# Windowed attention in the last layer: each pair of 7x7 windows placed at partitions 0 and 64, with one image row of windows as the unit of work

## The chip, the cores and the metric

The kernel runs on one core of one Trainium2 chip. A core has five engines that run on their own instruction streams: TensorE (PE in the profile, with its weight loads shown apart as PEld), VectorE (DVE), ScalarE (ACT), GpSimd (POOL) and SyncE (SP), which here only issues DMA transfers. They meet through semaphores. The metric is the device time of one execution in microseconds (us); lower is better.

## The reference

The program is four layers on a tensor x of 4 images, 56 x 56 positions, 256 channels, each of the form x = x + f(groupnorm(x)). The change concerns the last layer only, which is attention in shifted 7 x 7 windows with 8 heads of 32 channels:

```python
xs = jnp.roll(x, (-3, -3), axis=(1, 2))
xw = xs.reshape(B, 8, 7, 8, 7, C).transpose(0, 1, 3, 2, 4, 5).reshape(B * 64, 49, C)
qkv = (xw @ qkv_weight.T + qkv_bias).reshape(B * 64, 49, 3, 8, 32).transpose(2, 0, 3, 1, 4)
q, k, v = qkv[0] * 32 ** -0.5, qkv[1], qkv[2]
attn = jnp.einsum('whnd,whmd->whnm', q, k) + bias          # one 49 x 49 block for a window and a head
attn = softmax(attn + mask_of_the_window)
out = jnp.einsum('whnm,whmd->wnhd', attn, v).reshape(B * 64, 49, C) @ proj_weight.T + proj_bias
return roll_back(out)                                       # and x + this
```

All of it is in 32-bit floats. A window has 49 positions, an image has 8 x 8 windows, and the 4 images together have 32 rows of 8 windows.

## The kernel before

The four layers run one after another; the last one, `layer3`, fills the span from about 3430 us to its end at 3978 us. Inside it the program order of TensorE, VectorE, ScalarE and GpSimd is the order in which the source issues their instructions (`run(3, ...)` fixes these four engines); only the DMA queue is left to the planner. Activations lie with the channels on partitions, 2 halves of 128 channels by 392 positions for a row of 8 windows.

A row r goes through these steps:

- `prepare(r)` normalises the loaded x into `xn`: six VectorE instructions (line 939) and one small copy on ScalarE (line 2023).
- `project_rows(r)` makes keys and queries. Each of its four steps (keys, queries for the first 128 channels, then for the second) is two TensorE matmuls of 392 columns into a one-bank PSUM tile `ps_m` (line 945), and one ScalarE instruction that takes the result out (line 2035 for keys, 2039 for queries). There are two `ps_m` tiles, used in turn, so the third product in a sequence can't start before the first has been taken out.
- `values(r)` makes the values in two steps, a=0 with two position tiles and a=1 mostly with one (line 971); VectorE adds the bias (line 975), the result goes to DRAM, and `gather` reads it back by windows.
- attention, in `attend_quads`. Its unit is one row and one group of four heads (`quad(r, hq)`, 64 units). Two windows of 49 positions are handled as one piece of 98 by 98. The logits (line 1012) have the 98 keys on the partitions of PSUM: four heads stand in four 32-row groups of TensorE, so a matmul uses 32 rows and 98 columns. Half of every 98 x 98 piece belongs to two different windows and is masked off. Heads 0 and 1 go to PSUM tile s0, heads 2 and 3 to s1. ScalarE exponentiates s1 (line 1016) and GpSimd multiplies it by an exponentiated mask (line 1019); VectorE adds the mask to s0 (line 1017) and ScalarE exponentiates the sum (line 1018). The products with the values and with a matrix of ones (line 1027) use 98 rows and 32 columns, with the four heads in four column groups, and fill the PSUM tile `o`, of which there is one. `finish` takes the reciprocal of the sums (line 2075), lets GpSimd add it up for a later check (`seen`, line 985), and multiplies (line 2077).
- `project_out(r)` makes two more products like those of the projections, taken out by ScalarE (line 2097) and added to x on GpSimd (line 2099).

The loop of `attend_quads` is a pipeline of one unit. For a unit it issues the logits and the mask and exponentials, then `done()`, which is `finish` of the unit whose products came last, then `fill`, which is a share of the projections of row r+1, the values of row r+2, the output of row r-2 and the preparing of row r+3, and then the products of the unit before. The fill of a unit is one step of `project_out`, two of `project_rows` and one of `values`; the second unit of a row adds `prepare`. So on VectorE the mask addition of a unit stands ahead of the reciprocal.

The additive masks of this layer are made earlier in the run by `table_steps`, kept in DRAM (`m3d`) and loaded once into `m3`.

Of the kernel before, what the change touches and what calls it, by code (L numbers as in the profile page):

```python
# [24 lines left out]
FP = mybir.dt.float32  # L25
# [6 lines left out]
NIMG = 4  # L32
S = 56
T = S * S
C = 256
# [11 lines left out]
G2 = S // 2  # L47
WN = 49
WC = 8 * WN
GN_EPS = 1e-5  # L50
LN_EPS = 1e-5
TINY = 1e-12
# [84 lines left out]
def _constants():  # L137
# [47 lines left out]
    for lastrow in range(2):  # L185
        for lastpair in range(2):
            for w in range(2):
# [3 lines left out]
                if lastpair and w == 1:  # L191
# [2 lines left out]
                m3[sl, 2 * lastrow + lastpair, sl] = np.where(  # L194
                    part[:, None] != part[None], -100.0, 0.0)
    c["c_m3"] = m3
    return c


# [631 lines left out]
def direct_blocks(ctx: ExitStack, tc: tile.TileContext, d: dict, watch):  # L831
# [161 lines left out]

    def attend_quads(pool, units):

        def logits(w):
            nk, nq, nu = w["nk"], w["nq"], len(w["pieces"])
            w["first"]()
            s = [psum_tile(f"s{a}", 1, 2) for a in range(2)]
            for u, (k, q, *_) in enumerate(w["pieces"]):  # L1010
                for j in range(4):
                    nc.tensor.matmul(s[j // 2][:nk, j % 2, u * nq:(u + 1) * nq], lhsT=k(j), rhs=q(j),  # L1012
                                     start=True, stop=True)
            w["e"] = [pool.tile([P, 2, w["width"]], FP, tag=f"e{a}", name=f"e{a}", bufs=2) for a in range(2)]
            ev = [e[:nk, :, :nu * nq] for e in w["e"]]
            nc.scalar.activation(ev[1], s[1][:nk, :, :nu * nq], AF.Exp, accum_out=w.get("sum"))  # L1016
            nc.vector.tensor_tensor(ev[0], s[0][:nk, :, :nu * nq], w["mask"].to_broadcast([nk, 2, nu * nq]), ALU.add)
            nc.scalar.activation(ev[0], ev[0], AF.Exp)
            nc.gpsimd.tensor_tensor(ev[1], ev[1], w["emask"].to_broadcast([nk, 2, nu * nq]), ALU.mult)  # L1019

        def products(w):
            nk, nq = w["nk"], w["nq"]
            for k in range(2):
                for u, (_, _, v, start, stop) in enumerate(w["pieces"]):
                    po = w["o"](k, u)
                    for j in range(4):
                        nc.tensor.matmul(  # L1027
                            po[j * HD:(j + 1) * HD], lhsT=ones[:nk, :HD] if k else v(j),
                            rhs=w["e"][j // 2][:nk, j % 2, u * nq:(u + 1) * nq], start=start, stop=stop)

        held, done = None, no_step
        for w in units:
            logits(w)
            done()
            w["fill"]()
            if held:
                products(held)
                done = held["done"]
            held = w
        done()  # L1040
        products(held)
        held["done"]()


    def attend_pairs(pool, units):
# [870 lines left out]

    m3d = dram.tile([98, 2, NH, 4, 98], FP, name="m3d")

    def table_steps(big, pool):

# [8 lines left out]
        tab = big.tile([P, 2, NH], FP, name="tab")  # L1931
        nc.sync.dma_start(out=tab[:, 0], in_=d["table"][:P])
        nc.sync.dma_start(out=tab[:NR - P, 1], in_=d["table"][P:])
        t3 = big.tile([98, 4, 98], FP, name="t3")
        nc.sync.dma_start(out=t3, in_=d["c_m3"])
        base = big.tile([98, NH, WN], FP, name="base")

        def look_up(q0):
            idxf = pool.tile([P, NQ, WN], FP, tag="idxf", name="idxf")
            nc.vector.tensor_copy(idxf, idx[:, q0:q0 + NQ, :])  # L1940
            hot = pool.tile([P, 2, NQ * WN], FP, tag="hot", name="hot")
            for a, n in ((0, P), (1, NR - P)):
                nc.vector.tensor_scalar(hot[:n, a, :], idxf[:n].rearrange("p q k -> p (q k)"),
                                        rowf[:n, a:a + 1], None, ALU.is_equal)
            pb = ps_m()
            for a, n in ((0, P), (1, NR - P)):
                nc.tensor.matmul(pb[:NH, :NQ * WN], lhsT=tab[:n, a, :], rhs=hot[:n, a, :], start=(a == 0), stop=(a == 1))
            tb = pool.tile([NH, NQ, 98], FP, tag="tb", name="tb")
            for w in range(2):
                nc.vector.tensor_copy(tb[:, :, w * WN:(w + 1) * WN], pb[:NH, :NQ * WN].rearrange("p (q k) -> p q k", k=WN))  # L1950
            pt = ps_m()
            for q in range(NQ):
                nc.tensor.transpose(pt[:98, q * NH:(q + 1) * NH], tb[:, q, :], ident[:NH, :NH])
            nc.vector.tensor_copy(base[:, :, q0:q0 + NQ], pt[:98, :NQ * NH].rearrange("p (q h) -> p h q", h=NH))

        def mask(ty):
            m = pool.tile([98, NH, 98], FP, tag="m3", name="m3")
            for w in range(2):
                sl = slice(w * WN, (w + 1) * WN)
                nc.vector.tensor_tensor(m[:, :, sl], base, t3[:, ty:ty + 1, sl].to_broadcast([98, NH, WN]), ALU.add)  # L1960
            mv = m.rearrange("p (q j) k -> p q j k", j=4)[:, :, 2:4]
            nc.scalar.activation(mv, mv, AF.Exp)
            for pair in [3] if ty % 2 else range(3):
                nc.sync.dma_start(out=m3d[:, ty // 2, :, pair, :], in_=m)

        return [lambda q=q: look_up(q) for q in range(0, WN, NQ)] + [lambda ty=ty: mask(ty) for ty in range(4)]

# [11 lines left out]
    def layer3(early, big, pool, brief):  # L1979
# [16 lines left out]

        load(0)
        w_qkv = weight(early, "wqkv3", 3 * C)
        m3 = big.tile([98, 2, NH, 4 * 98], FP, name="m3l")
        nc.sync.dma_start(out=m3, in_=m3d.rearrange("p a h w k -> p a h (w k)"))  # L2000
        w_p = weight(pool, "wp3", C)

        def parts(win, x):
# [22 lines left out]
        def project_rows(r):  # L2026
            at = left(r % 8, WC)
            xn = xns.pop(r)[:, :, at:at + WC]
            qT = pool.tile([P, CC, WC], FP, tag="q", name="q3")
            kT = pool.tile([P, CC, WC], FP, tag="k", name="k3")  # L2030
            qk[r] = qT, kT

            def keys(m):
                pm = project(w_qkv, C + m * P, lambda h: xn[:, h, :], WC)
                nc.scalar.activation(kT[:, m, :], pm, AF.Identity, bias=bk3[:, m:m + 1])

            def queries(m):
                pm = project(w_qkv, m * P, lambda h: xn[:, h, :], WC)
                nc.scalar.activation(qT[:, m, :], pm, AF.Identity, bias=qbias[:, 2, m:m + 1], scale=SCALE)

            return [lambda f=f, m=m: f(m) for m in range(2) for f in (keys, queries)]

        def gather(r):

            b, c = divmod(r, 8)
            vs[r] = pool.tile([98, 4, C], FP, tag="v", name="v3")
            nc.sync.dma_start(out=vs[r], in_=vd[b][c * WC:(c + 1) * WC, :].rearrange("(k p) c -> p k c", p=98))

        def values(r):

# [9 lines left out]
                    gather(r)  # L2060
            return [lambda a=a: step(a) for a in range(2)]

        def quad(r, hq):
            b, wr = divmod(r, 8)
            qT, kT = qk[r]
            box = {}

            def output(k, u):
                if k + u == 0:
                    box["o"] = psum_tile("o", 1, 2)  # L2070
                return box["o"][:, k, u * 98:(u + 1) * 98]

            def finish():
                rs = pool.tile([P, WC], FP, tag="rs", name="rs3")
                nc.vector.reciprocal(rs, box["o"][:, 1, :WC])  # L2075
                seen(rs)
                nc.vector.scalar_tensor_tensor(attns[r][:, hq, :], box["o"][:, 0, :WC], 1.0, rs, ALU.mult, ALU.mult,
                                               accum_out=watch[2][:, 2 * r + hq:2 * r + hq + 1])

            def piece(u):  # L2080
                sl = slice(u * 98, (u + 1) * 98)
                return (lambda j: kT[hr(j), hq, sl], lambda j: qT[hr(j), hq, sl],
                        lambda j: vs[r][:, u, (4 * hq + j) * HD:(4 * hq + j + 1) * HD], True, True)

            mk = m3[:, wr // 7, 4 * hq:4 * hq + 4, :]
            i = 2 * (NIMG * 8 + r) + hq
            return dict(pieces=[piece(u) for u in range(4)], nk=98, nq=98, width=WC, mask=mk[:, 0:2, :],
                        emask=mk[:, 2:4, :], sum=watch[2][:98, i:i + 1], o=output, first=no_step, done=finish)

        def project_out(r):  # L2090
            x = pool.tile([P, CC, WC], FP, tag="xr", name="xr3")
# [12 lines left out]
        def stream():  # L2104
            n = NIMG * 8
            for r in range(n):
# [1 line left out]
                rows = lazily(project_rows, r + 1, 4) if r + 1 < n else []  # L2108
                ahead_values = lazily(values, r + 2, 2) if r + 2 < n else []
                out = project_out(r - 2) if r > 1 else []  # L2110
                for hq in range(CC):
                    steps = out[hq:hq + 1] + rows[2 * hq:2 * hq + 2] + ahead_values[hq:hq + 1]
                    if hq and r + 3 < n:
                        steps.append(lambda r=r: prepare(r + 3))
                    steps.append(step_stats)
                    w = quad(r, hq)
                    w["fill"] = lambda steps=steps: [f() for f in steps]
                    yield w

        prepare(0)  # L2120
        prepare(1)
# [3 lines left out]
        for step in project_rows(0):  # L2125
            step()
        prepare(2)
        attend_quads(pool, stream())
        for r in range(NIMG * 8 - 2, NIMG * 8):
            for step in project_out(r):  # L2130
                step()

# [122 lines left out]
```

## Time and profile before

| what | value |
|---|---|
| device time, median of 3 runs | 3989.01 us (3976.07 to 3992.41) |
| span of the profiled execution, first to last instruction | 3977.8 us |
| TensorE busy over the span | 3814.5 us (96%) |
| VectorE / ScalarE / GpSimd busy | 60% / 35% / 44% |
| the last layer | about 3430 to 3978 us |
| its steady part | 3461 to 3924 us |
| one row of windows there | 15.6 us |

The span counts from the first to the last instruction; the device time has some 11 us more around it. The chain of work that ended last names, for each stretch of time, the instruction on which the end depended. A line of the timeline gives start, duration, engine, source line, operation, tiles and count; in brackets stands how long the engine was idle before it and what released it. One 32-bit matmul of the source appears as two matmul records and two weight loads[...].

### The profile page before, as it was taken

The page shows a single profiled execution, that of the slowest core. Times are in us where ns is not written, and L with a number is a line of the kernel's source. Part 1 is how long each engine was busy: PE and PEld are TensorE (multiplying, and loading weights), DVE is VectorE, ACT ScalarE, POOL GpSimd, SP SyncE. Part 2 cuts the span into 40 slices and gives each one's busy share as a digit, 9 for nine tenths or more (in the row PEclk, how much of TensorE's full clock was granted, in tenths as well). Part 3 has the DMA queues.
Part 4 walks back from the last instruction along what each step waited for, and adds up shares of the span by engine and source line. Part 5 has one row for each costly group of instructions (what it writes and reads, how often), then busy time and mean ns, then how long its engine had stood idle before and what let it go on. Part 6 is the DMA issues. An engine that isn't in the chain of part 4 may idle for free. (4 is left out here: it accounts for less than half of the span.)

```text
span 3977.8 us, 92350 instructions
## 1 busy us (share of the span) xinstructions
PE 3814.5 (96%) x38871; PEld 2707.4 (68%) x38871; DVE 2372.2 (60%) x4431; ACT 1381.2 (35%) x2927; POOL 1745.8 (44%) x1883
## 2 busy tenths in 40 slices
PE   7999999889999999999999999999999999899998
PEld 4566666557777677776777767776676666566765
DVE  6777777734345544445444553446788887666665
ACT  3455545422222222222222222222555555344443
POOL 3566767721123312233112331123677777555554
PEclk9899999989999999999999999999999999999999
DMA  8343333320000100001000000001344443434442
GB/s 270 104 134 119 113 120 104 99 104 1 24 19 24 40 6 15 20 25 35 6 24 15 25 24 10 10 10 56 111 125 126 125 121 111 157 120 135 127 128 93
DMA packets 268659, 301.84 MB, mean 76 GB/s; under 512 B 25926, under 2 KB 260584, under 8 KB 267752
## 3 DMA queue, kind: packets, MB, share of 16 engines
q1 hardware_dynamic: 267946, 295.76, 23.9%
q8 instruction: 308, 5.05, 0.5%
q14 instruction: 117, 0.96, 0.1%
q10 hardware_dynamic: 288, 0.08, 0.0%
HBM read 203.39 MB, written 92.37 MB: 74 GB/s over the span
## 5 line engine op out<-in xcount | busy, mean ns | idle before, releaser
L1441 DVE TENSOR_TENSOR acc<-acc,ps_v 128x257 f32<-128x257 f32 x1104 | 463.4, 423 | 718.7 <-PE ps_v L1519 690.7
L1519 PE MATMUL ps_v<-xw,e 128*128 128x257 f32 x2208 | 612.6, 382 | 1.2 <-DVE acc L1441 1.2
L1514 PE MATMUL ps_o<-xw,at 128*128 128x257 f32 x2208 | 609.0, 379 | 0.0
L1409 PE MATMUL ps_s<-xnT,xd 128*128 128x512 f32 (+3 forms) x1344 | 572.7, 549 | 3.9 <-DVE xnT L1387 3.9
L1519 PEld LDWEIGHTS ps_v<-xw,e 128*128 128x128 f32 x2208 | 413.5, 189 | 142.7 <-issue 82.4
L1503 ACT COPY at<-ps_t 128x512 f32<-128x512 f32 (+3 forms) x332 | 170.6, 514 | 970.0 <-PE ps_t L1500 969.7
L1078 POOL TENSOR_TENSOR b<-e 126x336 f32<-126x336 f32 (+5 forms) x512 | 500.0, 997 | 9.6 <-ACT e L1066 1.5
L1514 PEld LDWEIGHTS ps_o<-xw,at 128*128 128x128 f32 x2208 | 419.1, 190 | 60.1
L945 PE MATMUL ps_m<-xn,w_wqkv 128*128 128x392 f32 x1024 | 379.1, 504 | 12.3 <-DVE dv L922 3.9
L1402 POOL TENSOR_SCALAR xd<-xnT,vec 128x128 f32<-128x128 f32 x192 | 116.8, 619 | 569.3 <-PE ps_s L1409 565.7
L1069 POOL TENSOR_TENSOR e<-e,m0t 126x672 f32<-126x672 f32 (+3 forms) x128 | 238.6, 1864 | 265.8 <-ACT e L1068 245.4
L1069 POOL TENSOR_TENSOR e<-e,bias 119x784 f32<-119x784 f32 (+5 forms) x128 | 244.0, 1906 | 179.9 <-ACT e L1068 178.6
L1409 PEld LDWEIGHTS ps_s<-xnT,xd 128*128 128x128 f32 x1344 | 225.8, 191 | 141.8 <-issue 126.5
L1412 ACT ACTIVATE e<-ps_s 128x512 f32<-128x512 f32 x336 | 185.4, 552 | 347.8 <-PE ps_s L1409 340.8
L990 ACT ACTIVATE no<-rs 128x168 f32<-128x168 f32 (+2 forms) x256 | 93.8, 367 | 583.8 <-DVE rs L1841 268.3
L945 PEld LDWEIGHTS ps_m<-xn,w_wqkv 128*128 128x128 f32 x1024 | 187.8, 191 | 137.3 <-ACT pr L2097 17.5
L1087 PEld LDWEIGHTS ps_o<-e,vp 124*32 124x32 f32 (+3 forms) x8192 | 177.8, 111 | 147.4 <-issue 97.7
L1087 PE MATMUL ps_o<-e,vp 124*32 124x112 f32 (+3 forms) x8192 | 242.0, 254 | 6.2 <-POOL e L1069 4.4
L1841 DVE RECIPROCAL rs<-ps_o 128x196 f32<-128x196 f32 (+2 forms) x128 | 176.0, 1375 | 87.1 <-PE ps_o L1087 86.6
L939 DVE TENSOR_SCALAR xn<-x,gst 128x28 f32<-128x28 f32 (+4 forms) x368 | 207.5, 616 | 32.3 <-PE ps_m L945 22.9
L1066 ACT ACTIVATE e<-e 126x672 f32<-126x672 f32 (+5 forms) x256 | 219.5, 857 | 20.7 <-DVE e L1065 8.0
L1019 POOL TENSOR_TENSOR e<-e,m3l 98x784 f32<-98x784 f32 x64 | 118.3, 1848 | 217.9 <-ACT e L1016 217.9
(196 smaller groups left out, 6293.8 us busy)
## 6 DMA issues: line engine op xcount, KB each, us to landing
x<-xr SPq DMA_DIRECT2D x64, 392.0 KB
x<-in_x SPq DMA_DIRECT2D x53, 448.0 KB
x<-x SPq DMA_DIRECT2D x60, 392.0 KB
xr<-x SPq DMA_DIRECT2D x60, 392.0 KB
vd<-v SPq DMA_DIRECT2D x72, 256.0 KB
xr<-in_x SPq DMA_DIRECT2D x32, 392.0 KB
xr<-x SPq DMA_DIRECT2D x28, 448.0 KB
x<-xr SPq DMA_DIRECT2D x28, 448.0 KB
```

The costliest lines, as they stand in the source:

```text
L939: nc.vector.tensor_scalar(dst, src, gst[:, h, 0:1], gst[:, h, 1:2], ALU.subtract, ALU.mult)
L945: nc.tensor.matmul(pm[:, :n], lhsT=w[:, h, col:col + P], rhs=rhs(h), start=(h == 0), stop=(h == CC - 1))
L1066: nc.scalar.activation(ev, ev, AF.Exp)
L1069: nc.gpsimd.tensor_tensor(parts(ev), parts(ev), w["emask"], ALU.mult)
L1078: nc.gpsimd.tensor_tensor(w["b"][a][:nk, :, :2 * nq].rearrange("p h (i c) -> p h i c", i=2), ev[:, :, :, 0, :], ev[:, :, :, 1, :], ALU.add)
L1087: nc.tensor.matmul(w["o"](k, i)[j * HD:(j + 1) * HD], lhsT=ones[:nk, :HD] if k else v(j, u), rhs=w["b"][j // 2][:nk, j % 2, i * nq:(i + 1) ...
L1409: nc.tensor.matmul(s[:, :n], lhsT=xd[j][:, h, :], rhs=xnT[:, h, first * P:last * P], start=(h == 0), stop=(h == CC - 1))
L1412: nc.scalar.activation(e[:, :n], s[:, :n], AF.Exp, scale=5.0)
L1441: nc.vector.tensor_tensor(acc[:, i, :], acc[:, i, :], pv[:, :C + 1], ALU.add)
L1514: nc.tensor.matmul(out[j][:, :C + 1], lhsT=e[:, col(i)] if i == j else at[:, col(i)], rhs=xw[:, i, :], start=(i == j), stop=(i == NB - 1))
L1519: nc.tensor.matmul(pv[:, :C + 1], lhsT=e[:, col(i)], rhs=xw[:, j, :], start=True, stop=True)
L1841: nc.vector.reciprocal(rs.rearrange("p (t c) -> p t c", t=2), pv[:, :, 1, :])
```

## The change

The two windows of a pair no longer form one 98 x 98 piece. Each window's 49 keys are a block of their own, the first four windows of a row at partitions 0 to 48 and the last four at partitions 64 to 112. The logits of a window and a head are a matmul of 32 rows, 64 columns (49 keys and 15 that aren't used) and 49 moving columns, and the products one of 49 rows, 32 columns and 49 moving columns. The number of these matmuls doubles, and each has half the moving columns. The blocks that belong to two windows are no longer computed, so both groups of four heads of a row fit in the tiles that one group filled, and the unit becomes a whole row: the mask addition, the multiplication and the exponentials run once a row instead of twice. The products and `finish` are still made in two halves, one for each group of four heads.

The order in the loop becomes: logits; `done()`; mask and exponentials; the first fill (keys, queries, keys and the first step of values); the first half of the products and its `finish`; the second fill (both steps of the output, queries, the second step of values, `prepare`); the second half of the products.

```diff
+HALF = 64
+WK = HALF + WN
-    def attend_quads(pool, units):
+    def attend_rows(pool, units, last_fill):
         def logits(w):
...
+            w["s"] = s = [psum_tile(f"s{a}", 1, 2) for a in range(2)]
+            for hq in range(CC):
+                for i in range(4):
+                    for u in range(2):
+                        for j in range(4):
+                            nc.tensor.matmul(s[j // 2][u * HALF:(u + 1) * HALF, j % 2, hq * WC // 2 + i * WN:hq * WC // 2 + (i + 1) * WN],
+                                             lhsT=w["k"](hq, j, 4 * u + i), rhs=w["q"](hq, j, 4 * u + i), start=True, stop=True)
+
+        def exponentials(w):
+            w["e"] = [pool.tile([P, 2, WC], FP, tag=f"e{a}", name=f"e{a}", bufs=2) for a in range(2)]
+            ev, sv = ([t[:WK, :, :WC] for t in w[n]] for n in ("e", "s"))
+            nc.scalar.activation(ev[1], sv[1], AF.Exp, accum_out=w["sum"])
+            nc.vector.tensor_tensor(ev[0], sv[0], w["mask"], ALU.add)
             nc.scalar.activation(ev[0], ev[0], AF.Exp)
-            nc.gpsimd.tensor_tensor(ev[1], ev[1], w["emask"].to_broadcast([nk, 2, nu * nq]), ALU.mult)
+            nc.gpsimd.tensor_tensor(ev[1], ev[1], w["emask"], ALU.mult)
+
+        def products(w, hq):
+            w["o"] = o = psum_tile("o", 1, 2)
             for k in range(2):
+                for i in range(4):
+                    for u in range(2):
+                        keys = slice(u * HALF, u * HALF + WN)
+                        for j in range(4):
+                            nc.tensor.matmul(
+                                o[hr(j), u, k * 256 + i * WN:k * 256 + (i + 1) * WN],
+                                lhsT=ones[keys, :HD] if k else w["v"](keys, i, 4 * hq + j),
+                                rhs=w["e"][j // 2][keys, j % 2, hq * WC // 2 + i * WN:hq * WC // 2 + (i + 1) * WN], start=True, stop=True)
 
         held, done = None, no_step
         for w in units:
             logits(w)
             done()
-            w["fill"]()
+            exponentials(w)
+            w["fill"](0)
             if held:
-                products(held)
-                done = held["done"]
+                products(held, 0)
+                held["done"](held, 0)
+            w["fill"](1)
+            if held:
+                products(held, 1)
+                done = lambda held=held: held["done"](held, 1)
             held = w
         done()
-        products(held)
-        held["done"]()
+        products(held, 0)
+        held["done"](held, 0)
+        last_fill()
+        products(held, 1)
+        held["done"](held, 1)
...
-                for hq in range(CC):
-                    steps = out[hq:hq + 1] + rows[2 * hq:2 * hq + 2] + ahead_values[hq:hq + 1]
-                    if hq and r + 3 < n:
-                        steps.append(lambda r=r: prepare(r + 3))
-                    steps.append(step_stats)
-                    w = quad(r, hq)
-                    w["fill"] = lambda steps=steps: [f() for f in steps]
-                    yield w
+                steps = [rows[:3] + ahead_values[:1], out + rows[3:] + ahead_values[1:]]
+                if r + 3 < n:
+                    steps[1].append(lambda r=r: prepare(r + 3))
+                w = row(r)
+                w["fill"] = lambda hq, steps=steps: [f() for f in steps[hq] + [step_stats]]
+                yield w
```

Around it, `finish` reads and writes the same 392 columns in two halves of 196, since `o` now has one bank for each of the two partition halves; the key tiles become two fixed ones with 15 spare columns set to zero; the values are gathered by two DMAs into partitions 0 and 64, with three buffers instead of two; and the mask table is built, stored and loaded in the new layout:

```diff
+        kts = [big.tile([P, CC, WC + HALF - WN], FP, name=f"k3_{i}") for i in range(2)]
+        for t in kts:
+            nc.gpsimd.memset(t[:, :, WC:], 0.0)
-            vs[r] = pool.tile([98, 4, C], FP, tag="v", name="v3")
-            nc.sync.dma_start(out=vs[r], in_=vd[b][c * WC:(c + 1) * WC, :].rearrange("(k p) c -> p k c", p=98))
+            vs[r] = pool.tile([P, 4, C], FP, tag="v", name="v3", bufs=3)
+            for u in range(2):
+                t0 = c * WC + u * WC // 2
+                nc.sync.dma_start(out=vs[r][u * HALF:u * HALF + WN], in_=vd[b][t0:t0 + WC // 2, :].rearrange("(k p) c -> p k c", p=WN))
-    m3d = dram.tile([98, 2, NH, 4, 98], FP, name="m3d")
+    m3d = dram.tile([WK, 2, 4, CC, 4, WN], FP, name="m3d")
```

## The prediction

> **What bounds the kernel now.** I read the busy times by stage first, then the timeline of two units, then the waits of the steady part. By stage (columns: length, then busy us and instructions of PE, PEld, DVE, ACT, POOL, then granted TensorE clock, DMA share, GB/s):
>
> ```profile
> 3461.00:3924.00 463.00, 462.43 (x6680) 321.74 (x6677) 318.15 (x477) 205.87 (x381) 241.82 (x285) 1.00 0.40 124
> 3924.00:3978.00 54.00, 36.68 (x571) 24.70 (x569) 25.19 (x32) 14.39 (x25) 25.54 (x38) 0.81 0.24 75
> ```
>
> In the steady part of the last layer TensorE has no idle time at full clock: its order is the time. So what the change takes from TensorE counts in full, and so does any new wait of TensorE. One unit and its neighbours in the timeline:
>
> ```profile
> 3689.31 0.89 PE L1027 MATMUL ps_o<-e,v 98*32 98x98 f32 x32
> 3689.42 0.42 DVE L975 TENSOR_TENSOR vt<-ps_m,bc 128x256 f32<-128x256 f32 x1 [0.85 <-PE ps_m L971]
> 3689.76 1.66 DVE L939 TENSOR_SCALAR xn<-x,gst 128x343 f32<-128x343 f32 x6
> 3690.02 0.86 PE L1027 MATMUL ps_o<-e,ones 98*32 98x98 f32 x32
> ...
> 3690.81 0.95 PE L1012 MATMUL ps_s<-q,k 32*98 32x98 f32 x32
> ...
> 3691.69 1.58 PE L945 MATMUL ps_m<-attn,w_wp 128*128 128x392 f32 x4
> 3691.86 0.97 DVE L1017 TENSOR_TENSOR e<-ps_s,m3l 98x784 f32<-98x784 f32 x1 [0.44 <-PE ps_s L1012]
> ...
> 3692.75 2.60 DVE L2075 RECIPROCAL rs<-ps_o 128x392 f32<-128x392 f32 x1
> ...
> 3692.87 0.86 ACT L1018 ACTIVATE e<-e 98x784 f32<-98x784 f32 x1
> ...
> 3693.63 0.57 ACT L2097 ACTIVATE pr<-ps_m,vec 128x392 f32<-128x392 f32 x1
> 3694.63 0.59 ACT L2035 ACTIVATE k<-ps_m,vec 128x392 f32<-128x392 f32 x1 [0.42 <-PE ps_m L945]
> ...
> 3695.39 0.57 DVE L2077 SCALAR_TENSOR_TENSOR attn<-ps_o,rs 128x392 f32<-128x392 f32 x1
> ```
>
> The reader is to see the order on VectorE and ScalarE: the mask addition (L1017) goes ahead of the reciprocal, so the second exponential (L1018) is over 2 us after the logits, and ScalarE is then free to take the first projection out of `ps_m`. From the waits of the steady part (total us, times, longest):
>
> ```profile
> PEld ps_m L945 <- ACT pr L2097: 16.9, 56, 0.6
> ```
>
> Even now TensorE's weight load waits for ScalarE there in every unit, 0.3 us, just hidden behind the matmul that is still running. So this release has no slack.
>
> [...] the records of L1027 start at 0, 7, 13 and 20 ns and then 84 ns after the first[...]. [...]
>
> ```profile
> 3943.00:3946.50 3.50, 0.67 (x6) 0.10 (x8) 3.25 (x4) 1.48 (x4) 2.52 (x2) 1.00 0.23 59
> 3947.70:3951.10 3.40, 3.40 (x49) 2.38 (x39) 1.22 (x2) 1.13 (x3) 0.57 (x3) 0.50 0.00 0
> ```
>
> An idle stretch of 2.8 us from 3943.6 on is followed by 3.4 us at clock 0.50. In the matmul records of the whole span I count 12 gaps of over 2.5 us, each followed within some 4 us by a stretch at 0.50, and 11 of 1.5 to 2.3 us, of which 3 or 4 are.
>
> **The change, part by part.** A row is now two units, 15.63 us by the starts of its matmuls: twelve projections of four records, 0.329 us a record, values, 2 x 0.88 logits, 2 x 1.50 products, and the switches between tile shapes, 0.1 to 0.2 us each, inside these numbers.
>
> *TensorE's work.* Products: groups of four records 84 ns apart for 98 columns, 16 groups a unit. After: twice the records, half the columns, eight tiles (two row groups by four column groups). [...] starting eight at 6.7 ns takes 54. I take 54: 16 x 54 + 90 for the switch = 0.95 us a half. Logits: groups 86 ns apart, after 16 groups a row; [...] 16 x 59 + 160 = 1.10 us. Saving 2 x 0.55 + 0.66 = 1.76 us a row. Bounds: no trace here has eight tiles at once. [...] If eight tiles do no better than four, products take 1.5 to 1.6 and logits 2.0 us, nothing is saved.
>
> *VectorE, ScalarE, GpSimd.* Once a row instead of twice: mask addition 0.97, two exponentials 0.82 and 0.86, multiplication 1.85 us. None of them bounds the stage, so this saves nothing by itself. Masks, the half as large load of `m3`, zeroed key columns, the second gather DMA and the third buffer of `v`: once, or on queues with slack; nothing. If gathers came late they would be seen at the products, but these run a whole row later.
>
> *The new wait.* The order is now logits, `done()`, exponentials, fill. So the reciprocal and its multiplication stand ahead of the mask addition on VectorE, the second exponential waits for that, and ScalarE can't take any projection out before it. With two `ps_m` tiles the third product of the first fill (keys of the second half) then waits. Queued behind it are the rest of TensorE's row. From the first record of a row's last products, with the durations above, and with the steps of the second fill ahead of them on VectorE as they stand now:
>
> - VectorE: bias addition +0.11, normalising +0.45 to +2.1 (it isn't waiting for anything), reciprocal +2.15, multiplication +4.8, mask addition +5.4, done +6.35.
> - ScalarE: second exponential +6.4, first keys taken out +7.17 to +7.75.
> - TensorE: products to +0.95, logits to +2.05, keys and queries 1.42 + 1.32 to +4.8, then nothing until +7.8. A stall of 3.0 us.
>
> After it come keys 1.42, values 1.82, products 0.95, both outputs 2.74, queries 1.32, values 0.96: 9.2 us. These meet no wait: the first half's reciprocal and multiplication (3.2 us) fit beside the 5 us of the second fill. The row is 7.8 + 9.2 = 17.0 us, +1.4. Faster products don't help here: up to +7.8 their time is inside the stall. If eight tiles bring nothing, the stall is 1.6 us and the row 17.6.
>
> *The clock.* 3.0 us of idle TensorE in each row are above the 2.5 us that were always followed by half clock. One window of 3.4 us at half costs 1.7 us of work; it costs less if it begins in the gap, more if a second one follows. I take 1.7. Bounds 0 and 3.4.
>
> *Sum.* The wait stands in rows 2 to 30 (no reciprocal is due ahead of it before, and no keys are made after): 29 x (1.4 + 1.7) = 90. The other rows and the end, where fewer units wait for each other's reciprocal in series, give some 6 back. +84 us. The profiled execution's 3977.8 us of span and some 11 around it are the median, 3989.0; I forecast 4073.
>
> **The rivals.**
> 1. *Stall without half clock*, or with the stall shortened to under 2.3 us by slow tiles: 29 x 1.4 to 2.0 less 3 to 6 gives +35 to +58, 4024 to 4047. For it: gaps up to 2.3 us mostly left the clock alone. Against: the sum says 3.0.
> 2. *No stall, the saving counts*: if the mask addition were not held by the reciprocal, or ScalarE's turn came in time, 31 rows x 1.76 = 55 us less: 3934, with the bounds 3925 to 3965. For it: TensorE is the bound, and its matmul work really shrinks. Against: the order in the source, and VectorE and ScalarE kept that order before. It decides if the reciprocal starts so early that ScalarE is free by +4.8, 3 us sooner than in my sum.
> 3. *Starved TensorE*: 256 instead of 128 instructions stand in each half of the products and again in the logits; if they can't be supplied at some 4 ns each, with the trace's densest 128 at 10.8 ns [...], at 8 ns products take 2.0 and logits 2.0. Up to +7.8 the stall swallows this; the other half adds 1.1: 29 x 2.5, about +70, without half clock. 4060, on the same side as the forecast.
>
> **How the numbers follow.** Forecast with half clock 0.60 (4040 to 4125), rival 1 0.18, rival 3 0.06, rival 2 0.13, others near no change 0.03. A measurement of this kernel can't tell less than 0.5%, 20 us, from no change. Faster by more than that is rival 2, 0.13; within it the rest and the low edge of rival 1, 0.05; slower 0.82. The range 4012 to 4125 takes in the bounds of the clock's cost but for its extremes, and rivals 1 and 3; it leaves out rival 2.
>
> **What would show it.** Right: TensorE busy clearly under 0.9 in the steady part, a wait of about 3 us a row of `ps_m` L945 for ScalarE's keys, the mask addition right after the multiplication of `finish`, the granted clock well below 1.00, a row near 18.7 us. Eight tiles: groups of eight records 46 to 59 ns apart. Wrong: TensorE without gaps there, or waits at the products or the gather instead.

## The result and the profile after

The changed kernel takes 4258.1 us (median of 5 runs, 4245.47 to 4265.0) beside 3976.8 us for the kernel before (5 runs, 3975.68 to 3992.41). The ratio is 1.069, with a 95% interval of 1.067 to 1.071: 281 us slower, where 84 were forecast. The profiled execution took 4258.8 us and has a span of 4257.0 us, so the device time has 1.8 us around the span. The 11 us given above came from two different executions, and the forecast of 4073 us starts some 12 us too high.

The page of the changed kernel, the span in 40 slices of 106 us (busy tenths of TensorE, its clock, and the DMA share):

```profile
PE   6728998979999999999999999999999994888887
...
PEclk9759999989999999999999999999999998999998
DMA  7114333331000100001000000003444432333332
```

TensorE has holes in two places. From the 35th slice on, the last layer, it is at 8 tenths instead of full: that is the stage that the prediction speaks of. But slices 2, 3 and 34 are at 7, 2 and 4, and they lie outside the part that was forecast to change. Those holes (stretches in which TensorE does nothing) are four stops, of 45.1 us at 186, 10.7 at 240, 56.8 at 265 and 51.7 at 3572 us. Two of them and the steady part of the last layer, by stretch (columns as in the prediction: length, busy us and instructions of PE, PEld, DVE, ACT, POOL, then clock, DMA share, GB/s):

```profile
186.00:226.00 40.00, 0.00 (x0) 0.00 (x0) 0.00 (x0) 0.00 (x0) 0.00 (x0) 0.52 0.08 11
3572.00:3622.00 50.00, 0.01 (x1) 0.00 (x0) 0.00 (x0) 0.00 (x0) 0.00 (x0) 0.55 0.16 56
3645.00:4190.00 545.00, 476.92 (x12048) 324.68 (x12050) 291.14 (x441) 152.91 (x286) 181.27 (x250) 0.94 0.34 105
```

In the two stops shown no engine computes, and the DMA share is 0.08 to 0.16, about 1.3 to 2.6 of 16 engines. So everything waits for transfers that nearly all DMA engines leave alone. In the last line TensorE is idle for 68 of 545 us, where before it was idle for half a microsecond of 463.

The first logits of the last layer start at 3641.1 us; before, at 3460.1. From there to the end of the span it is 615.8 us, before 517.6. So 181 us were lost ahead of the last layer's attention, in the stops above all (164 us), and 98 us inside it. These are two losses, and they are taken one after the other.

**The stops.** SyncE in the timeline of the changed kernel at the first stop (start, length of the issue, line, transfer, count):

```profile
179.07 47.23 SPq L1984 DMA_DIRECT2D m3d<-m  x4
...
226.40 19.00 SPq L987 DMA_DIRECT2D vd<-v  x1
229.56 0.36 DVE L1981 TENSOR_TENSOR m<-base,t 113x196 f32<-113x196 f32 x1 [44.78 <-DMA m3d<-m]
229.84 0.74 DVE L983 TENSOR_TENSOR v<-ps_m,bc 64x256 f32<-64x256 f32 x2
...
230.72 1.83 PE L953 MATMUL ps_m<-xn,w_wk 128*128 128x448 f32 x2 [45.09 <-DVE v L983]
```

Four stores of the mask table to `m3d` keep SyncE for 47 us, and the next transfer is held for 19 more. VectorE waits until the stores have freed the buffer of `m`, TensorE's next result waits in PSUM behind that on VectorE, and TensorE stands for 45 us. The load of the table, at 3562 us, does the same to the transfers behind it:

```profile
3562.29 0.27 SPq L2020 DMA_DIRECT2D m3l<-m3d  x1
3569.74 14.47 SPq L1900 DMA_DIRECT2D x<-xr  x1
3584.30 7.44 SPq L1894 DMA_DIRECT2D xr<-x  x1
```

The two transfers behind it, of 392 KB each, take 14.5 and 7.4 us to issue, and the two after those 16.2 together; one ahead of it, at 3561.83, took 0.36. The records of the single DMA packets show how few engines work: of the stores' 7232 packets never more than two are under way at once, and the load's 113 packets go nearly one by one from 3564.6 to 3619.8 us. In the kernel before, with 98 rows, up to 24 packets of the stores are under way at once, and the load takes 9.5 us.

**The last layer.** The hole of one row, in the timeline of the changed kernel:

```profile
3814.12 0.47 PE L1021 MATMUL ps_s<-q,k 32*64 32x49 f32 x32
...
3815.15 2.59 DVE L2095 RECIPROCAL rs<-ps_o 128x392 f32<-128x392 f32 x1
...
3816.37 1.21 PE L1021 MATMUL ps_s<-q,k 32*64 32x49 f32 x96 [1.78 <-issue]
...
3818.27 0.97 DVE L1028 TENSOR_TENSOR e<-ps_s,m3l 113x784 f32<-113x784 f32 x1
...
3820.03 0.57 ACT L2058 ACTIVATE k<-ps_m,vec 128x392 f32<-128x392 f32 x1
...
3820.66 1.58 PE L953 MATMUL ps_m<-xn,w_wqkv 128*128 128x392 f32 x4 [0.25 <-ACT k L2058]
```

The order on VectorE and ScalarE is the predicted one, and `ps_m` does wait for ScalarE's keys, but for 0.25 us here. The hole stands elsewhere: in the middle of the logits, after 32 of 128 records, TensorE stops for 1.78 us and the profile shows nothing that it waited for ("issue"). The waits of TensorE from 3645 to 4190 us (total us, times, longest) say the same of all rows:

```profile
PE ps_s L1021 <- issue: 52.2, 27, 2.9
...
PE ps_m L953 <- ACT k L2058: 6.5, 12, 1.6
```

What TensorE lacks there is instructions. They arrive on a DMA queue of their own (q8, of the kind "instruction" on the page), in blocks: the page of the changed kernel has 355 packets and 5.82 MB there, 16.4 KB a packet (before: 308 and 5.05 MB). In the records of this queue a block starts at 3814.03 us and has landed at 3814.99; the hole ends at 3816.37, 1.38 us later. So it is everywhere: the changed kernel has 35 holes of over 0.8 us in logits and products, 67 us in sum, and they end 1.41 us after a block has landed (median). For 33 of them the profile shows no wait for another engine or a DMA; over all kernels there are 174 such holes, and nine in ten of them end 1.24 to 1.57 us after a block.

Where the holes stand says the same. Count TensorE's records (matmuls, weight loads and semaphore instructions) from the first one kept, in stretches of 256. Of the 174 holes, 171 end just before record 193 or 194 of a stretch (counted from 0), all 33 of the changed kernel among them, and when such a hole ends, exactly as many blocks have landed as whole stretches have been counted. So TensorE stops at the edge of a block and goes on with the block that has just come. In the kernel before, every block of the last layer lands at least 5.1 us before its first record starts, and there are no such holes. In none of the 13 traces do two blocks start closer than 3.1 us.

A row's second half of products and the logits after it are 512 instructions, two blocks, that TensorE would get through in some 3 us (1.3 and 1.5 us without a hole).

### The profile page after: what moved, and what is told of

The parts are those of the page before. It is cut to its first block, busy times and chain, and to the rows that moved or that the text cites. A ratio compares the mean times of both kernels' runs of the same rounds, so it can differ in the third digit from the quotient of the medians.

```text
span 4257.0 us, 104562 instructions
## 1 busy us (share of the span) xinstructions
PE 3857.7 (91%) x45015; PEld 2726.9 (64%) x45015; DVE 2349.4 (55%) x4399; ACT 1327.6 (31%) x2831; POOL 1685.1 (40%) x1860
## 3 DMA queue, kind: packets, MB, share of 16 engines
q8 instruction: 355, 5.82, 0.6%
## 5 line engine op out<-in xcount | busy, mean ns | idle before, releaser
L953 PE MATMUL ps_m<-xn,w_wqkv 128*128 128x392 f32 x1024 | 414.4, 540 | 19.4 <-ACT k L2058 6.5
L953 PEld LDWEIGHTS ps_m<-xn,w_wqkv 128*128 128x128 f32 x1024 | 198.7, 204 | 159.9 <-issue 34.1
L979 PE MATMUL ps_m<-w_wqkv,xn 128*128 128x256 f32 (+1 forms) x800 | 205.5, 395 | 55.0 <-DVE xr L1897 51.7
```

The costliest lines, as they stand in the source:

```text
L953: nc.tensor.matmul(pm[:, :n], lhsT=w[:, h, col:col + P], rhs=rhs(h), start=(h == 0), stop=(h == CC - 1))
L979: nc.tensor.matmul(pm[:k, j * C:(j + 1) * C], lhsT=xn[:, h, first:first + k], rhs=w[:, h, :], start=(h == 0), stop=(h == CC - 1))
```

## The experiments

The times are medians of a kernel's runs, and each ratio is taken to runs of the kernel before that stood beside it (medians of 3976.8 to 3980.3 us). The other columns are sums of TensorE's work over the last layer in one profiled execution, by the starts of its matmuls, so that a hole counts to the group it stands in (us; a dash where it wasn't summed):

| kernel | time, us | ratio to before (95%) | logits | products | keys, queries | last layer |
|---|---|---|---|---|---|---|
| before | 3976.8 | 1 | 56.9 | 101.8 | 164.7 | 517.6 |
| changed | 4258.1 | 1.0692 (1.0671 to 1.0713) | 112.7 | 99.4 | 206.6 | 615.8 |
| before_113 | 4243.0 | 1.0675 (1.0657 to 1.0692) | - | - | - | 515.5 |
| before_112 | 3984.5 | 1.0005 (0.9995 to 1.0015) | - | - | - | 517.1 |
| rows128 | 4095.4 | 1.0295 (1.0278 to 1.0312) | 116.4 | 104.4 | 215.1 | 632.1 |
| swap | 4100.3 | 1.0317 (1.0300 to 1.0335) | 122.5 | 106.9 | 196.8 | 620.3 |
| spread | 4067.7 | 1.0234 (1.0217 to 1.0251) | 53.3 | 122.0 | 173.2 | 590.3 |
| ones | 4049.1 | 1.0173 (1.0157 to 1.0188) | 82.8 | 78.9 | 213.8 | 570.7 |
| best | 3987.5 | 1.0017 (1.0010 to 1.0024) | 66.9 | 74.2 | 170.1 | 511.4 |
| best_no_swap | 4006.4 | 1.0064 (1.0050 to 1.0078) | 63.4 | - | 188.4 | 528.4 |
| best_no_ones | 4063.4 | 1.0216 (1.0200 to 1.0232) | 80.3 | 117.1 | 175.8 | 582.6 |
| apart | 3967.8 | 0.9969 (0.9957 to 0.9980) | 50.1 | 79.0 | 172.9 | 496.3 |
| apart_masks | 3954.3 | 0.9930 (0.9916 to 0.9944) | 50.4 | 78.5 | 172.8 | 495.1 |

The theory after the result had two parts. The stops: transfers of 113 rows aren't shared out among the DMA engines as those of 98 rows are. That is the author's reading of the two traces, with at most two packets of the stores under way at once in the changed kernel and up to 24 in the kernel before; they don't show what makes the difference. The holes: instruction supply, against the prediction's wait for ScalarE as the rival.

### rows128: the mask table with 128 partitions

```diff
-WK = HALF + WN
+WK = 2 * HALF
-            nc.gpsimd.memset(tb[:, :, WN:HALF], 0.0)
+            nc.gpsimd.memset(tb.rearrange("p q (w k) -> p q w k", w=2)[:, :, :, WN:], 0.0)
```

> One-engine theory: the two stops of the first layer (45 and 57 us, with a smaller one of 11) and the stop of 52 us at the start of the last layer come from transfers of the mask table whose 113 partition rows, [...] are not shared out among the DMA engines. With the table laid out on 128 rows all of them go: 165 to 185 us less than the changed kernel, so 4073 to 4093 us, and the steady rows of the last layer stay at some 18.5 us. Rival, short packets: the stores are slow since their rows are 196 bytes instead of 392. Then the stops of the first layer stay (some 4200 us), and only the load, whose rows are 12.5 KB, may change.

4095.4 us, 163 less than the changed kernel, and just above the 4073 to 4093 that were expected. The issues of the stores (shortest, median and longest in ns, then first and last start), first of the changed kernel and then of rows128:

```profile
L1984 SPq DMA_DIRECT2D m3d<-m x8: 244/14220/19074, 179.1 to 302.1; - x8
```

```profile
L1984 SPq DMA_DIRECT2D m3d<-m x8: 386/568/1487, 173.0 to 194.3; - x8
```

The stops are gone with more bytes to move and rows of the same 196 bytes, so it was the row count: now up to 29 packets of the stores are under way at once, and the load's 128 packets take 5.6 us. The first logits stand at 3474.7 us, still 14.6 later than before. The last layer is no better, 632 us. TensorE's order of work is the same in the changed kernel, rows128 and swap (below), and it came to 616, 632 and 620 us there; most of that difference goes with the granted clock (93, 120 and 104 us at half clock, of which half is lost). The profiled execution of rows128 was also 13 us longer than its median run.

### before_113 and before_112: the row count alone

In the kernel before, only the number of partitions of the table's tiles was changed, and the added rows are set to zero; nothing of the attention changes.

```diff
-    m3d = dram.tile([98, 2, NH, 4, 98], FP, name="m3d")
+    m3d = dram.tile([113, 2, NH, 4, 98], FP, name="m3d")
-            m = pool.tile([98, NH, 98], FP, tag="m3", name="m3")
+            m = pool.tile([113, NH, 98], FP, tag="m3", name="m3"); nc.gpsimd.memset(m[96:], 0.0)
...
-        m3 = big.tile([98, 2, NH, 4 * 98], FP, name="m3l")
+        m3 = big.tile([113, 2, NH, 4 * 98], FP, name="m3l")
```

> The kernel before, with 15 idle rows added to the mask table (98 to 113) and nothing else. One-engine theory: it takes the same kind of stops, 100 us or more in the first layer and, with a load twice as large as that of the changed kernel, 50 to 100 us at the start of the last layer; together 150 to 220 us more than before, 4130 to 4200 us. Rival, short packets (these rows stay at 392 bytes): under 20 us more than before.

> The kernel before, with 14 idle rows added to the mask table (98 to 112[...]) instead of 15. One-engine theory: 112 rows are shared out, so under 15 us more than before, against the 266 us of 113 rows. Rival: the cost of before_113 came with the added rows or the clearing of them, which differ by one row only; then it stays near 4240 us.

113 rows cost 266 us, more than the 150 to 220 that were expected; 112 rows cost 4 us, which can't be told from none. The issues of the stores in before_113 and in before_112:

```profile
L1964 SPq DMA_DIRECT2D m3d<-m x8: 249/21960/23977, 167.9 to 312.9; - x8
```

```profile
L1964 SPq DMA_DIRECT2D m3d<-m x8: 331/624/1683, 169.8 to 193.1; - x8
```

and two of the three stops of before_113:

```profile
184.00:264.00 80.00, 0.00 (x0) 0.00 (x0) 1.42 (x3) 0.53 (x1) 4.09 (x5) 0.51 0.11 24
...
3601.00:3703.00 102.00, 0.38 (x2) 0.00 (x0) 0.00 (x0) 0.00 (x0) 0.00 (x0) 0.53 0.11 38
```

One row fewer and they are gone, though the added rows are set to zero there too. The stops are longer than in the changed kernel because this table holds the masked-off halves too (2401 KB are loaded in the kernel before, 1384 KB in the changed one). The last layer is untouched, so the row count accounts for the first loss and has no part in the second.

### swap: the mask and exponentials ahead of `done()`

All further kernels are rows128 with more edits.

```diff
             logits(w)
+            exponentials(w)
             done()
-            exponentials(w)
```

> The layout of 128 rows, and the mask and exponentials put ahead of done(), as they were before. ScalarE theory (the prediction's): TensorE's wait for the keys' exit from PSUM goes, 1.5 to 3 us a row, 45 to 90 us less than rows128. Instruction theory: the wait in a row is the supply of instructions to TensorE during the logits, and ScalarE's turn lies beside it: 0 to 20 us less than rows128, and the gaps of some 2 us inside the logits stay.

This is the test of the predicted wait, and it gains nothing: 5 us slower than rows128, with runs of 4099 to 4110 us against 4093 to 4109. TensorE's waits from 3645 us to the end in rows128, then in swap:

```profile
PE ps_s L1021 <- issue: 43.1, 21, 3.2
...
PE ps_m L953 <- ACT k L2058: 3.9, 3, 1.8
```

```profile
PE ps_s L1021 <- issue: 44.5, 21, 3.5
```

The wait for ScalarE is gone, and its place in the sum was 4 us. While TensorE stands in the logits, VectorE's reciprocal runs (in the row of the changed kernel shown above from 3815.15 to 3817.74 us, across the hole); by the time the logits are done the stall that was predicted behind them has already passed beside the hole.

### spread: both output steps between the second half of the products and the logits

```diff
-                steps = [rows[:3] + ahead_values[:1], out + rows[3:] + ahead_values[1:]]
+                steps = [rows[:3] + ahead_values[:1], rows[3:] + ahead_values[1:], out]
...
                 done = lambda held=held: held["done"](held, 1)
+            w["fill"](2)
             held = w
```

> The layout of 128 rows, and both output projections moved from ahead of a row's last products to behind them, so that 2.7 us of long matmuls stand between the 256 instructions of these products and the 256 of the logits. Instruction theory: the gaps inside the logits shrink from about 2 us to under 0.7, and the half clock that follows them goes: 50 to 90 us less than rows128. ScalarE theory: the wait moves by the same 2.7 us, so this also gains, and is told apart by swap; the gaps inside the logits would stay then.

28 us faster than rows128, where 50 to 90 were expected. The outputs are 16 instructions that take 2.9 us, so the blocks have time to come: the logits lose nearly all their holes (116.4 to 53.3 us). But what was between the two halves of the products is now short, and TensorE's waits from 3480 to 4020 us show what came in its place:

```profile
PE ps_o L1039 <- DVE attn L2098: 29.2, 26, 2.0
PE ps_o L1039 <- issue: 24.9, 13, 3.1
```

The second half needs `o`, and the first half's `finish` takes 3.2 us on VectorE; 2.3 us of work lie between. And the holes went to the products, whose two halves are now closer together.

### ones: fewer instructions in the products

The four matmuls of a 49-column block each with the matrix of ones become one with 196 columns, since the ones are the same for all windows. This takes 96 of 256 instructions from each half.

```diff
                         for j in range(4):
+                            if k:
+                                if i == 0:
+                                    nc.tensor.matmul(o[hr(j), u, 256:256 + WC // 2], lhsT=ones[keys, :HD],
+                                                     rhs=w["e"][j // 2][keys, j % 2, hq * WC // 2:(hq + 1) * WC // 2], start=True, stop=True)
+                                continue
```

> The layout of 128 rows, and the products with the matrix of ones made as 8 matmuls of 196 columns in a half instead of 32 of 49; a half is then 160 instructions of TensorE instead of 256, with the same columns. Instruction theory: a half goes from 1.32 to some 0.9 us, and since its burst with the logits is 416 instructions instead of 512, the gaps in the logits shrink: 40 to 70 us less than rows128. ScalarE theory: the shorter products only lengthen TensorE's wait for the keys; 0 to 25 us less.

46 us faster than rows128. A half's products take 1.14 us instead of 1.32 (0.9 was expected), and the holes of over 0.8 us fall from 74 to 32 us although the same columns are computed in the same order. TensorE's waits from 3480 to 4010 us:

```profile
PE ps_m L953 <- ACT k L2063: 31.4, 24, 2.3
PE ps_s L1021 <- issue: 26.9, 20, 2.0
```

With the holes smaller the predicted wait comes out: 31 us in 24 waits, up to 2.3 us a time.

### best, best_no_swap, best_no_ones: the three edits together, and without one

best is ones and swap with the second output step behind the last products (`steps = [rows[:3] + ahead_values[:1], out[:1] + rows[3:] + ahead_values[1:], out[1:]]`); the other two leave out one edit each.

> All together: 128 rows, products with ones in 8 matmuls, mask and exponentials ahead of done(), and the second output projection alone moved behind a row's last products (the first stays ahead, so that the finish of the first half has 3.7 us). Instruction theory: a row is twelve projections 7.9, values 2.8, two halves 1.9, logits 1.5, switches 0.3: 14.4 us instead of the 15.6 of the kernel before, so 30 to 50 us less than that kernel, some 3930 to 3950 us. If gaps remain in the logits or the products, it stays above the kernel before.

> As best, with done() ahead of the mask and exponentials. With the gaps in the logits gone, the prediction's wait of TensorE for ScalarE should show: normalising, reciprocal, multiplication, mask addition and exponential end some 7.7 us after the start of the last products, TensorE needs the bank at 6.5: 1.2 us a row, 15 to 45 us more than best. If the order never matters: within 5 us of best.

> As best, with the products with ones in 32 matmuls of 49 columns. Two halves cost 0.8 us a row more, 25 us; if 1.4 us of long matmuls between 256 and 256 instructions aren't enough for the supply, gaps of some 1 us come back as well, and it is 40 to 70 us above best.

best came to 3987.5 us, 7 more than before, and missed the 3930 to 3950 that were expected: a row takes 15.3 us instead of 14.4, and the logits 67 us where they take 50 without holes. Its last layer is 6 us shorter than that of the kernel before, while the first logits come 12 us later. The edits are worth 19 us (swap) and 76 us (ones) here, where swap alone on rows128 was worth nothing; the 76 are above the 40 to 70 that were expected. TensorE's waits from 3480 to 3930 us in best, then in best_no_swap:

```profile
PE ps_s L1021 <- issue: 7.8, 14, 1.5
...
PE ps_m L953 <- ACT k L2064: 0.5, 1, 0.5
```

```profile
PE ps_m L953 <- ACT k L2064: 11.5, 20, 0.9
```

So the predicted wait is real and is undone by the edit that should undo it, once there is no larger hole over it.

### apart and apart_masks: bursts kept apart, and fewer stores

apart is ones, so with `done()` first as in the changed kernel, and with the outputs behind the last products and one more projection between the halves. Each burst of small matmuls (a run of them with nothing else between) then has long matmuls ahead of it:

```diff
-                steps = [rows[:3] + ahead_values[:1], out + rows[3:] + ahead_values[1:]]
+                steps = [rows[:2] + ahead_values[:1], rows[2:] + ahead_values[1:], out]
```

In apart_masks the masks also go to DRAM once for each of the four types, in one store each with 1568 bytes in a row; one load brings them back to `mc`, and eight GpSimd copies spread them over `m3`.

```diff
-    m3d = dram.tile([WK, 2, 4, CC, 4, WN], FP, name="m3d")
+    m3d = dram.tile([WK, 4, 4, CC, WN], FP, name="m3d")
-            for pair in [3] if ty % 2 else range(3):
-                nc.sync.dma_start(out=m3d[:, ty // 2, :, :, pair, :], in_=m)
+            nc.sync.dma_start(out=m3d[:, ty], in_=m)
```

> 128 rows, products with ones in 8 matmuls, done() ahead of the mask and exponentials as in the changed kernel, and the fills shared out anew: keys, queries and the first values ahead of the first half, keys, queries and the second values ahead of the second half, both output projections behind it. Every burst of 160 or 256 instructions then has 2.8 to 4.5 us of long matmuls ahead of it, and the finish of the second half lies beside the output projections. Instruction theory: logits 1.47 us in nearly all rows, a row of 14.6 to 14.9 us, 10 to 20 us less than best, 3965 to 3980 us. If done() ahead of the exponentials still holds ScalarE, TensorE waits for the keys' exit and it is above best.

> As apart, and the mask table kept in DRAM once for each of its four types, in rows of 1568 bytes a partition instead of 196, and spread to the eight places by GpSimd copies after the load. The stores' packets in the first layer go from 8192 to 2048, so the stop of some 7 us there and the later start of the last layer (3472 against 3460 us in the kernel before) should go: 5 to 15 us less than apart. If that start has another cause, no change from apart within 3 us.

Both beat the kernel before, apart by 12.5 us and apart_masks by 26 us (0.993, 0.9916 to 0.9944): no run of either is as long as the shortest of the 21 runs of the kernel before beside them, 3974.8 us. By stretch, apart_masks from 3480 to 3925 us:

```profile
3480.00:3925.00 445.00, 441.42 (x9657) 286.25 (x9659) 294.32 (x441) 154.97 (x288) 185.12 (x261) 1.00 0.43 130
```

TensorE is full again at full clock, but for 3.6 of 445 us, and a row takes 14.8 us. Of the holes for which the profile shows no other wait two are left, 4 us. That `done()` first no longer costs anything is seen in the timeline of apart_masks:

```profile
3714.54 2.60 DVE L2104 RECIPROCAL rs<-ps_o 128x392 f32<-128x392 f32 x1
...
3716.49 1.54 PE L1021 MATMUL ps_s<-q,k 32*64 32x49 f32 x128
...
3717.18 0.57 DVE L2106 SCALAR_TENSOR_TENSOR attn<-ps_o,rs 128x392 f32<-128x392 f32 x1
...
3718.11 0.97 DVE L1028 TENSOR_TENSOR e<-ps_s,m3l 128x784 f32<-128x784 f32 x1 [0.35 <-PE ps_s L1021]
```

The outputs stand ahead of the logits, so the multiplication ends at 3717.75, before the logits do, and the mask addition waits for the logits (0.35 us) and not for `finish`. The logits have all their 128 records in one piece. The new layout of the table brings the first logits from 3473.7 us in apart to 3464.2, which is most of what was left of the first loss; VectorE's wait for the stores falls from 7.0 us to 0.7.

## Why the prediction was right on the side and wrong on the size

**The step that failed** is the sentence that put the masks and the load of `m3` at "once, or on queues with slack; nothing". It looked at bytes, which nearly halve, and not at the row count, which goes from 98 to 113. This term measured 163 us between the changed kernel and rows128, and 266 us in the kernel before. "Once" was no excuse: a single load held up four other transfers on SyncE's queue, and with them TensorE for 52 us.

**The last layer** was forecast at +84 us, with a row of 18.7 us; it is +98 us, with a row of 18.5. That is near the forecast by luck, as is the right side: neither of the two losses is the wait that was forecast. The forecast had a stall of 3.0 us on `ps_m` in each row; the changed kernel has 6.5 us of it in all, in 12 rows, and 27 holes in the logits between 3645 and 4190 us. So the third rival, starved TensorE, was what happened, and what failed is its sentence "Up to +7.8 the stall swallows this": the two lie one after the other on TensorE, and the earlier one, the hole, swallowed the stall. The stall was also priced too high: where holes are fewer or smaller it is 1.3 us a time in ones, and 0.6 in best_no_swap (11.5 us in 20), where one output step more lies ahead of it, not 3.0. The rival's price was wrong too, since it looked for a slower steady rate, while the supply came as a stop of some 2 us for every block that was late.

**The clock.** The forecast put 29 x 1.7 = 49 us on half clock. TensorE ran at half clock for 93 us of the last layer (before: 20), and half of the 73 us more, 37, is work lost; keys and queries, which follow the hole, took 42 us more than before. This term was of the right kind and nearly of the right size, though with the holes in the place of the stall.

**Eight tiles.** A half of the products was put at 0.95 us and takes 1.32; logits were put at 1.10 us a row and take 1.47 where there is no hole. In the records (medians of bursts without a hole) the first 32 of 128 products take 254 ns, 63 a group of eight, near the 54 that the forecast took; the 95 after them take 9.7 ns each, 78 a group. For logits it is 279 ns and then 11.0 ns each, 88 a group where the forecast took 59, the author's estimate, which no trace had shown. So the saving is 2 x 0.18 + 0.29 = 0.65 us a row instead of 1.76, and 1.01 with fewer instructions for the ones. apart_masks has 0.8 of it in its row.

**What cost nothing, as forecast.** Gathers in two DMAs, the third buffer of `v` and the zeroed columns: no wait of TensorE in any kernel here names them. A few of GpSimd's waits (5 to 8 us, once a kernel) name a gather, but TensorE doesn't wait there.

**Rival 2**, no stall and 55 us less than before, is what the layout could have given; with its order of work and its table mended, and fewer instructions for the ones, it gives 26 us less (3954).

**Two slips in the sums** change nothing in the forecast: a row holds six projections of four matmul records, not twelve, and the upper end of rival 1 is 29 x 2.0 less 3, +55 and not +58.

What stays open: why transfers of 113 rows had at most two packets under way at once where 98 and 128 rows had up to 24 and 29, and why two blocks of instructions don't come closer than 3.1 us. No run changed the supply itself; that it is the supply rests on the holes standing at the edges of blocks and ending a fixed time after a block has landed, and on their shrinking when instructions are taken out or bursts moved apart. Also open is what decides how often the clock falls, which differs (93 to 120 us at half clock) between kernels with the same order of TensorE's work.

## What to carry to other kernels

Twice the instructions for the same columns is a cost of its own: count TensorE's instructions in each burst, and put long matmuls between bursts, since here 512 in a row stopped TensorE for some 2 us. When a tile's partition count changes, look at every transfer that has it as its outer dimension; 113 rows there took 163 us that no instruction of the attention shows. And where two waits follow each other on one engine, undoing the hidden one tells nothing: it was worth 0 us at first and 19 us once the larger was gone.

## What the runs showed of the hardware

- Transfers of 113 rows ran at a DMA share of 0.08 to 0.16, and the stores among them held SyncE's issue for up to 24 us each (median 14 to 22); for stores of 98, 112 and 128 rows the median issue was 0.5 to 0.6 us. Of the changed kernel's stores, with 113 rows, never more than two packets were under way at once; with 98 rows up to 24, with 128 up to 29.
- Such a transfer held up the next ones on SyncE's queue already at their issue: 7 to 19 us instead of 0.36.
- TensorE's instructions came in blocks of 16.4 KB (256 records, by 171 of 174 holes) that started at least 3.1 us apart, and work went on 1.4 us after a late one had landed, at the edge of the block.
- With eight tiles a burst starts faster than it goes on: 7.9 ns a matmul record for the first 32 products and 9.7 after them, 8.7 and 11.0 for logits.
